# A two-layer convolution kernel: last 3x3 images brought to the points one by one, another order at the start of the 7x7 convolution, sums of two strips

## The chip, the cores and the metric

The kernel runs on one core of one Trainium2 chip. The core has five engines with an instruction queue each: TensorE (PE in the profile; its weight loads are PEld), VectorE (DVE), ScalarE (ACT), GpSimd (POOL) and SyncE (SP), which here only issues DMAs. Each engine works through its queue in order; semaphores make one wait for another. On-chip data lies in SBUF (128 partitions), TensorE writes to PSUM, which has eight banks of 512 float32 values per partition.

The metric is the device time of one execution, in microseconds (us). Times of one kernel agree within about 1%.

## The reference

Everything is float32. The input x is 4 images of 256 channels of 64x64.

```python
# layer 0: attention over 49 shifts
k = conv7x7(x, w1, dilation=2, pad=6) + b1        # 256 -> 128 channels
k = conv1x1(k, w2) + b2                           # 128 -> 49
attn = softmax(k, axis=1)                         # over the 49 shifts
x = sum over u, v in 7x7 of shifted(x, 2u, 2v) * attn[u, v]   # 256 channels
# layer 1: bottleneck with batch statistics
h = relu(bn(conv1x1(x, w1)))                      # 256 -> 64
h = relu(bn(conv3x3(h, w2, pad=1)))               # 64 -> 64
h = bn(conv1x1(h, w3))                            # 64 -> 256
out = relu(h + x)
```

`bn` takes mean and variance over all images and pixels, so every normalisation needs the whole layer before it.

## The kernel before

**7x7 convolution.** The two convolutions of layer 0 are one: the 7x7 weights are multiplied with the 1x1 weights (`product`, L320), so that the output has 49 channels. The seven rows of taps are done by interpolation: the input rows are combined into values at nine points (0, infinity, and plus and minus the four of `PAIRS`, L63), multiplied there, and combined back. The channels are two halves of 128 (`half` 0 and 1), the columns four strips of eight (`NS`, L68). There are five passes over the points (`passes`, L183), each with two values per pixel column (`xi`, i = 0 and 1). A pass visits each strip on VectorE (`visit`, L233, made of `even`, `odd` and `mix`, all through `stt`, L152), and then TensorE runs `column_convs` (L252, matmuls at L263), which adds into the PSUM banks `acc[i][s]` of the strip and its two neighbours. All five passes run for half 0; their sums go to DRAM (`put_aside`, L282). Then they run for half 1: `put_back` (L592) copies the sums into the banks, `column_convs` adds, and `outputs` (L569) combines the two banks of a strip into `logit`, once both neighbours are through.

**The beginning.** `piece(n, b)` (L345) loads some rows of image b and sorts them into `slots`: four copies per piece (`sort_x`, L161, two for each row parity k), all on ScalarE for even b and all on GpSimd for odd b. A ring of four `raw` tiles holds the pieces. `early(n)` (L351) is the visit of the first pass for the output rows that the pieces so far allow; `early(0)` and `early(1)` do all four strips at once, `early(2)` goes by strip. In between, seven products of half 0 fill seven PSUM banks, `bank[0]` to `bank[6]`, and ScalarE and VectorE empty them (L337 to L343). After that come the first `column_convs`, with the products of half 1 between strips 0, 1 and 2, and `apply_factor` (L227), which prepares `slots` for the second pass.

**Softmax and gather.** `exponents` and `shares` make the softmax; `turn` (L549) transposes the shares on TensorE and copies them to `amat` on ScalarE (L567), in the last turns also on VectorE. `load_xt` loads the input in another layout, `shift_xt` (L122) makes a copy shifted by half the partitions, and `gather` (L714) multiplies the two for 16 units of image and quarter. `conv1` (L758) is the first 1x1 convolution.

**3x3 convolution.** `relu1(slot)` (L887) normalises two images. One image of slot 0 is convolved directly (`direct`, L923); the other three are brought to six points along the row (`inputs`, L899, 12 sums on VectorE into the tiles `vs`), multiplied (`products`, L936, twelve matmuls each) and combined back. Each `vs` tile has room for two images. Then come the second normalisation, the moments for the third (L1002 to L1006), and the outputs (L1047 and L1051).

**Order.** In a `manual_schedule` block the engines named keep the order of the program. The first half of the 7x7 convolution is in such a block for VectorE and TensorE, its beginning also for ScalarE and SP, and the turns for VectorE, TensorE, ScalarE and SP. Elsewhere a scheduler sets the order on each engine.

Of the kernel before, what the change touches and what calls it, by code (L numbers as in the profile page):

```python
# [48 lines left out]
P = 128  # L49
# [44 lines left out]
def conv_seq_kernel(ctx: ExitStack, tc: tile.TileContext, xp, xt, w1, b1, w2t, b2, m1t, g1, be1,  # L94
# [63 lines left out]

    zero_rows(slots)

    def sort_x(copy, raw, b, r0, n, dst, w0):  # L161

        d = dst.rearrange("p k (w b e) i -> p k w b e i", b=B, e=Q)
        nw = d.shape[2]
        for k in range(2):
            m = r0 // 2 + (r0 // 2 + 3 + k) % 2
            count = ((r0 + n) // 2 - m + 1) // 2
            i = (m + 3) // 2
            for a in range(2):
                lo = 2 * m + a - r0  # L170
                copy(  # L171
                    d[:, k, :, PLACE[b], 2 * a : 2 * a + 2, i : i + count],
                    raw[:, lo : lo + 4 * count - 3 : 4, PAD + 2 * w0 : PAD + 2 * w0 + 2 * nw].rearrange(
                        "p r (w c) -> p w c r", c=2
                    ),
                )
# [47 lines left out]

        return row

    def apply_factor(t, factor, n, cols=slice(None)):  # L227

        for k in range(2):
            v = t[:, k, cols, :n]  # L230
            stt(v, v, -factor, t[:, k, cols, 1 : n + 1])

# [4 lines left out]
    def strip(s, n=1):  # L237
        return slice(SW * s, SW * (s + n))
# [37 lines left out]
    with ExitStack() as s1:  # L276
# [13 lines left out]
        with ExitStack() as s2:  # L290
# [54 lines left out]
            def piece(n, b):  # L345
                r0, k = PIECES[n]
                raw = rawp.tile([P, 24, WP], F32, tag="raw", name="raw")
                nc.sync.dma_start(out=raw[:, :k], in_=xp[b, :P, r0 : r0 + k, :])
                sort_x(nc.gpsimd.tensor_copy if b % 2 else nc.scalar.copy, raw, b, r0, k, slots, 0)

            def early(n, cols=slice(None), parts=(even, odd, mix)):  # L351

# [8 lines left out]
                if mix in parts:  # L361
                    mix(p, x0, x1)

            bank = [acc[i][s] for s in (2, 3, 0, 1) for i in range(2)]
            with tc.manual_schedule(engines={mybir.EngineType.Activation, mybir.EngineType.SP}):
                for b in range(B):
                    piece(0, b)
                w1a = load_w1(0)
                early(0)
                nc.scalar.copy(b1row, b1sb.to_broadcast([P, P]))  # L370
                nc.tensor.matmul(bank[7][:, :K], b1row, w2sb, start=True, stop=False)
                nc.tensor.matmul(bank[7][:, :K], ones, b2sb, start=False, stop=True)
                nc.scalar.copy(bias, bank[7][:, :K])
                for b in range(2):
                    piece(1, b)
                    product(w1a, 0, b, bank[b])
                for b in range(2, B):
                    piece(1, b)
                early(1, parts=(even,))
                for v in range(2, 5):  # L380
                    if v > 2:
                        piece(2, v - 3)
                    product(w1a, 0, v, bank[v])
                early(1, parts=(odd, mix))
                for v in range(5, K7):
                    piece(2, v - 3)
                    product(w1a, 0, v, bank[v])
                w1b = load_w1(1)
            for s in range(NS):
                early(2, strip(s))  # L390
            u = weights(0, 0)
            column_convs(0, u, True)
            for v in range(4):
                product(w1b, 1, v, bank[v])
                if v == 1:
                    apply_factor(slots, squares[0], NR - 1, strip(0, 2))
            column_convs(1, u, True)
            put_aside(0, 1)
            apply_factor(slots, squares[0], NR - 1, strip(2, 2))
            for v in range(4, K7):  # L400
                product(w1b, 1, v, bank[v - 2])
        for s in range(2, NS):
            column_convs(s, u, True)
            put_aside(0, s)
# [23 lines left out]
        def fill_stage(h):  # L428
            zero_rows(stage)
            for r0 in range(0, H, ROWS2):  # L430
                for b in range(B):
                    raw = rawp.tile([P, ROWS2, WP], F32, tag="raw", name="raw")
                    nc.sync.dma_start(out=raw, in_=xp[b, P:, r0 : r0 + ROWS2, :])
                    sort_x(nc.scalar.copy, raw, b, r0, ROWS2, stage, R // 2 * h)

        def stage_parts(h, strips=range(2)):
            for s in strips:
# [61 lines left out]
    smp = pool(ctx, "smp", 2)  # L499
    outer = pool(ctx, "outerp", 1).tile([P, OUTER], F32, name="outer")  # L500

    logit = outer[:, :LG].rearrange("p (s j v) -> p s j v", s=NS, j=4)
    combs = outer[:, LG : LG + 4 * WS * K].rearrange("p (n v) -> p n v", v=WS * K)
    n_combs = [0]

    pads = [outer[:, LG + PADS * i : LG + PADS * (i + 1)] for i in range(2)] + [arena[:, 11264 : 11264 + PADS]]
    pads = [t.rearrange("p (j w e) -> p j w e", j=4, w=4) for t in pads]
    bias_s = bias.unsqueeze(1).to_broadcast([P, WS, K])

    def columns(s, h):  # L510

        return logit[:, s].rearrange("p j (w k) -> p j w k", k=K)[:, :, 4 * h : 4 * h + 4, :]

    def exponents(s):

# [50 lines left out]
                else:  # L566
                    nc.scalar.copy(dst, src)  # L567

    def outputs(n, p, s):  # L569

        if p is None:
            for i, j, f in ((0, 0, 1.0 / d_zero), (1, 3, 1.0)):
                stt(logit[:, s, j, :], acc[i][s][:, : WS * K], f, logit[:, s, j, :])
            return
        d = 2.0 * p * p
        for q in PAIRS:
            if q != p:
                d *= p * p - q * q
        m, t = (combs[:, 2 * i + n_combs[0] % 2] for i in range(2))
        n_combs[0] += 1  # L580
        nc.scalar.copy(m, acc[0][s][:, : WS * K])  # L581
        nc.vector.tensor_tensor(t, acc[1][s][:, : WS * K], m, ALU.add)
        nc.vector.tensor_tensor(m, m, acc[1][s][:, : WS * K], ALU.subtract)  # L583
        for j in range(4):
            src, dst = (m if j % 2 else t), logit[:, s, j, :]
            if n == 0:
                dst, src = (v.rearrange("p (w k) -> p w k", k=K) for v in (dst, src))
                stt(dst, src, p**j / d, bias_s)
            else:
                stt(dst, src, p**j / d, dst)  # L590
# [10 lines left out]
    with tc.manual_schedule(engines={mybir.EngineType.SP}):  # L601
        for s in range(2):
            put_back(0, s)
        for s in range(NS):
            if s in (1, 2):
                load_ready(s + 1)
                put_back(0, s + 1)
                load_rows(s + 1)
            if s > 1:
                finish_parts(s)  # L610
            column_convs(s, weights(0, 1), False)
            for d in range(s - 1 if s else 0, s + 1 if s == NS - 1 else s):
                outputs(0, PAIRS[0], d)
    for n, (p, factor, left) in enumerate(passes):
        if n == 0:
            continue
# [6 lines left out]
        for s in range(NS):  # L623
            if n == 2:
                apply_factor(slots, factor, NR - 2, strip(s))
            if p is not None:
                visit(slots, strip(s), p, left)
            for d in ([s] if s == 0 else []) + ([s + 1] if s + 1 < NS else []):
                put_back(n, d)
            column_convs(s, u, False)  # L630
            for d in range(s - 1 if s else 0, s + 1 if s == NS - 1 else s):
                outputs(n, p, d)
            if p is None and 0 < s < NS - 1:
                if s == 2:
                    turn(0, 0)
                exponents(s - 1)
                shares(s - 1)
# [18 lines left out]
    with tc.manual_schedule(  # L656
# [5 lines left out]
        turn(1, 0)  # L662
        exponents(3)
        shares(2)
        load_xt(xtiles[1], *units[0], 1)
        turn(1, 1)
        turn(2, 0)
        shares(3)
        turn(2, 1, True)
        turn(3, 0, True)  # L670
        turn(3, 1, True)
    xts[(*units[0], 0)], xts[(*units[0], 1)] = xtiles[:2]
    more_xt(1)

    o = NH1
    w2blk = arena[:, o : o + 6 * P].rearrange("p (n m) -> p n m", m=P)
# [123 lines left out]
        if n + 2 < len(units):  # L800
            more_xt(n + 2)
    conv1(*units[-2], True)
    s_acc.close()


    pb_ = pool(ctx, "pb", 7, PSUM)
    pst = pool(ctx, "pst", 1, PSUM)
    yins = [arena[:, yin_at + C * 4 * i : yin_at + C * 4 * (i + 1)] for i in range(18)]
    yins += [bks.rearrange("p n v -> p (n v)")[:, : C * 4]]
    n_small = [yin_at + C * 4 * 18]  # L810
# [22 lines left out]
        nc.vector.tensor_tensor(sh, beta, sh, ALU.subtract)  # L833
        return sc, sh

    def from_stats(st, gamma, beta):

        mv, m = small(2), small(3)
        nc.vector.bn_aggr(mv, st.rearrange("p n s -> p (n s)"))
        pm = pst.tile([P, 3], F32, tag="pst", name="pm")  # L840
        nc.tensor.matmul(pm[:, :2], pavg_sb, mv, start=True, stop=True)
        nc.tensor.matmul(pm[:, 2:], pdiff_sb, mv[:, :1], start=False, stop=True, skip_group_check=True)
        nc.vector.tensor_copy(m, pm)
# [3 lines left out]
    def from_sums(sums, gamma, beta):  # L847

        t, m = small(2), small(2)
        nc.vector.tensor_reduce(t, sums, AX.X, ALU.add)  # L850
        pm = pst.tile([P, 3], F32, tag="pst", name="pm")
        nc.tensor.matmul(pm[:, :2], pavg_sb, t, start=True, stop=True)
        nc.vector.tensor_scalar(m, pm[:, :2], 1.0 / (B // 2 * H * W), None, ALU.mult)
        nc.vector.scalar_tensor_tensor(m[:, 1:2], m[:, 0:1], m[:, 0:1], m[:, 1:2], ALU.mult, ALU.subtract)
# [15 lines left out]
    for n in range(len(yins)):  # L870
        load_y(n)

    sc1, sh1 = from_stats(st1, bn12[:, 0:1], bn12[:, 1:2])

# [10 lines left out]
    def relu1(slot):  # L887
# [3 lines left out]
        h = h1[slot][:, :, :, :, 1 : T + 1]  # L891
        for a, r in ((0, 0), (1, R)):
            half = slice(a * MID, (a + 1) * MID)
            do(h[half, :, :, r], half)
        for g in range(2):
            for e in (1, 0):
                do(h[:, e::2, g, 1:R])
# [66 lines left out]
    direct(0, 0)  # L964
    inputs(0, slice(1, 2))
    relu1(1)
    products(0, 1)
    inputs(1, slice(0, 2))
    for g in range(2):
        products(1, g)  # L970

# [141 lines left out]
```

## Time and profile before

| | |
|---|---|
| median of 3 runs | 827.38 us (821.28 to 827.96) |
| the profiled execution | 826.64 us |
| its span, first to last instruction | 824.9 us |
| mean granted clock of TensorE | 0.96 |
| TensorE busy | 744.7 us, 90% |
| VectorE busy | 576.7 us, 70% |
| ScalarE busy | 294.9 us, 36% |
| GpSimd busy | 96.0 us, 12% |
| DMA | 150.27 MB, mean 182 GB/s |

The span in stages, as the timeline shows them: loading and the first products to 62.3 us; the first half of the 7x7 convolution to about 274; its second half to 463.9; softmax and turns to 506.5; gather and first 1x1 convolution to 667.8; first normalisation and 3x3 convolution to 740; moments and third normalisation to 774; outputs to the end.

The span in 40 equal slices of 20.6 us, each digit a busy share in tenths (9 is 90% or more):

```profile
PE   0919999999999999979999998999999969879994
DVE  5689979999577999999999764222323232964695
ACT  2430155112641012101111284343433364235497
PEclk9978999999999999989999999999999979898997
DMA  8930188924897893101200112566757587250298
```

And the chain of work that ended last, in shares of the span by engine:

```profile
PE 75%; DVE 10%; ACT 7%; DMA 4%; issue 3%; ACTq 1%; POOL 0%; SPq 0%; DVEq 0%
```

A busy share is a mean over stages with different limits. What an edit is worth is read from the stage in which it lies: which engine works there without a pause, and what ends the others' waits. In the lines of the timeline and the chain, the first number is the start in us from the span's beginning, the second the length, and then come engine, line of the code, operation and tiles.

### The profile page before, as it was taken

The numbers are of one execution on the slowest core, as the hardware profiler recorded it, in microseconds if no ns is written. First come the engines' busy times: TensorE is split into PE (matmuls) and PEld (weight loads), VectorE is DVE, ScalarE is ACT, GpSimd is POOL, SyncE is SP. The second block draws the span as 40 slices with busy tenths as digits, with TensorE's granted clock in tenths as the row PEclk, the third lists the DMA queues.
The fourth block names the chain that finished last, engine by engine and source line by source line (L and its number), as shares of the span: only waits on it lengthen the run. The fifth ranks groups of instructions, "written<-read, shape, count | busy, mean of one in ns | idle before, by whom it ended". The sixth has DMA issues, their size and how long they took to land.

```text
span 824.9 us, 10896 instructions
## 1 busy us (share of the span) xinstructions
PE 744.7 (90%) x4192; PEld 604.9 (73%) x4192; DVE 576.7 (70%) x697; ACT 294.9 (36%) x585; POOL 96.0 (12%) x149
## 2 busy tenths in 40 slices
PE   0919999999999999979999998999999969879994
PEld 0918988888888888768888888888888844338641
DVE  5689979999577999999999764222323232964695
ACT  2430155112641012101111284343433364235497
POOL 5630010001000010000004001222322200000000
PEclk9978999999999999989999999999999979898997
DMA  8930188924897893101200112566757587250298
GB/s 292 349 157 0 40 277 289 387 99 155 291 379 267 340 336 114 49 20 32 58 20 1 57 49 75 192 233 217 246 186 245 182 294 257 90 165 35 96 371 348
DMA packets 58950, 150.27 MB, mean 182 GB/s; under 512 B 7314, under 2 KB 35602, under 8 KB 54546
## 3 DMA queue, kind: packets, MB, share of 16 engines
q1 hardware_dynamic: 48624, 124.34, 42.9%
q10 hardware_dynamic: 10274, 25.23, 7.9%
q8 instruction: 33, 0.54, 0.3%
q14 instruction: 19, 0.16, 0.1%
HBM read 93.81 MB, written 55.74 MB: 181 GB/s over the span
## 4 chain that ended last, share of the span: by engine, by line
PE 75%; DVE 10%; ACT 7%; DMA 4%; issue 3%; ACTq 1%; POOL 0%; SPq 0%; DVEq 0%
PE acc L263 43%; PE acc L732 16%; DVE arena L152 5%; ACT outer L1051 4%; PE acc L766 4%; PE pdirect L930 3%; PE acc L326 3%; PE pconv L942 2%; PE moments L1006 2%; DVE outer L152 2%; DMA raw<-in_xp_dram 1%; PE acc L560 1%; ACT arena L567 1%; DMA bn<-in_g_dram 1%; PE pturn L1002 1%
## 5 line engine op out<-in xcount | busy, mean ns | idle before, releaser
L263 PE MATMUL acc<-arena 128*128 128x343 f32 (+4 forms) x2000 | 381.5, 353 | 25.9 <-DVE arena L152 25.9
L263 PEld LDWEIGHTS acc<-arena 128*128 128x128 f32 x2000 | 322.5, 192 | 83.8 <-issue 21.8
L152 DVE SCALAR_TENSOR_TENSOR arena<-arena 128x1024 f32<-128x1024 f32 (+6 forms) x184 | 292.3, 1626 | 23.6 <-PE acc L263 15.3
L732 PEld LDWEIGHTS acc<-arena,outer 128*128 128x128 f32 x1152 | 130.9, 194 | 9.1 <-issue 6.5
L732 PE MATMUL acc<-arena,outer 128*128 128x128 f32 (+1 forms) x1152 | 132.2, 278 | 2.3 <-ACT arena L567 2.3
L774 DVE BATCH_NORM_STATS2 st<-acc 128x6 f32<-128x512 f32 x16 | 11.1, 694 | 71.6 <-PE acc L766 71.6
L171 ACT COPY stage<-raw 128x128 f32<-128x128 f32 x128 | 43.7, 414 | 22.1 <-DMA raw<-in_xp_dram 20.7
L326 PE MATMUL acc<-powers,w1raw 128*128 128x196 f32 (+1 forms) x196 | 45.6, 396 | 6.0 <-DMA w1raw<-in_w_dram 6.0
L287 ACT COPY sv<-acc 128x392 f32<-128x392 f32 x40 | 19.2, 484 | 85.0 <-PE acc L263 68.9
L326 PEld LDWEIGHTS acc<-powers,w1raw 128*128 128x128 f32 x196 | 44.8, 315 | 6.3 <-DVE arena L152 6.1
L124 ACT COPY outer<-outer 64x2304 f32<-64x2304 f32 x15 | 31.7, 2111 | 31.2 <-DMA outer<-in_xt_dram 26.4
L152 DVE SCALAR_TENSOR_TENSOR outer<-outer 128x392 f32<-128x392 f32 (+3 forms) x67 | 38.4, 631 | 5.0 <-DMA arena<-y_dram 5.0
L989 PE MATMUL pconv<-arena,w3m 64*128 64x512 f32 x128 | 41.8, 638 | 0.0
L581 ACT COPY outer<-acc 128x392 f32<-128x392 f32 x16 | 7.7, 486 | 92.6 <-PE acc L263 73.8
L942 PE MATMUL pconv<-outer,arena 128*128 128x512 f32 x72 | 33.9, 633 | 4.1 <-DVE outer L152 4.1
L754 DVE COPY bks<-acc 128x256 f32<-128x256 f32 x32 | 12.1, 419 | 36.1 <-PE acc L732 36.1
L598 ACT COPY acc<-bks 128x392 f32<-128x392 f32 x40 | 19.3, 491 | 48.5 <-DVE outer L583 29.2
L989 PEld LDWEIGHTS pconv<-arena,w3m 64*128 64x128 f32 x128 | 19.1, 185 | 21.1 <-DVE arena L1047 15.8
L1051 ACT ACTIVATE outer<-arena 128x512 f32<-128x512 f32 x50 | 33.0, 750 | 3.7 <-DVE arena L833 1.4
L1047 DVE SCALAR_TENSOR_TENSOR arena<-pconv,arena 128x512 f32<-128x512 f32 x50 | 33.3, 740 | 0.0
L125 POOL COPY outer<-outer 64x2048 f32<-64x2048 f32 x15 | 28.3, 1885 | 41.3 <-DMA outer<-in_xt_dram 40.3
L567 ACT COPY arena<-acc 128x512 f32<-128x512 f32 x52 | 26.9, 718 | 13.9 <-PE acc L560 13.9
(142 smaller groups left out, 638.9 us busy)
## 6 DMA issues: line engine op xcount, KB each, us to landing
raw<-in_xp_dram SPq DMA_DIRECT2D x36, 608.0 KB, 5.6
out_dram<-outer ACTq DMA_DIRECT2D x16, 1024.0 KB, 4.1
outer<-in_xt_dram SPq DMA_DIRECT2D x17, 896.0 KB, 5.8
arena<-y_dram SPq DMA_DIRECT2D x25, 512.0 KB, 7.8
fsort_dram<-stage SPq DMA_DIRECT2D x2, 4864.0 KB, 15.1
arena<-fsort_dram SPq DMA_DIRECT2D x8, 1216.0 KB, 9.6
y_dram<-outer SPq DMA_DIRECT2D x16, 512.0 KB, 5.1
aside_dram<-sv ACTq DMA_DIRECT2D x40, 196.0 KB, 4.6
```

Source lines behind the costliest of these rows:

```text
L124: nc.scalar.copy(t[:MID], x[MID:])
L152: nc.vector.scalar_tensor_tensor(out, in0, scalar, in1, ALU.mult, ALU.add)
L171: copy(d[:, k, :, PLACE[b], 2 * a : 2 * a + 2, i : i + count], raw[:, lo : lo + 4 * count - 3 : 4, PAD + 2 * w0 : PAD + 2 * w0 + 2 * nw].r ...
L263: nc.tensor.matmul(acc[i][d][:, o : o + (hi - lo) * K], xi[:, i, CW * w : CW * w + CW, :].rearrange("p x t -> p (x t)"), u[i][:, lo * K : ...
L326: nc.tensor.matmul(pw[:, o : o + n], w1raw[:, :, u * K7 + v], powers[:, u, :n], start=(u == 0), stop=(u == K7 - 1), skip_group_check=True,)
L567: nc.scalar.copy(dst, src)
L732: nc.tensor.matmul(pt[:, o : o + hi - lo], x[:, i, half * P : (half + 1) * P], a[:, :, blocks, :].rearrange("p x m e -> p m x e"), start=( ...
L766: nc.tensor.matmul(pt[a * MID : (a + 1) * MID, :], w1m[:, n, :], ys[a, n][:, 512 * i : 512 * i + 512], start=(n == 0), stop=(n == NH - 1), ...
L942: nc.tensor.matmul(m[k], wu[:, k, j, :], vs[k][:, g, j : j + R, :], start=(j == 0), stop=(j == 1))
L989: nc.tensor.matmul(pt, w3m[part, half * P : (half + 1) * P], h2[part, slot, q, 512 * i : 512 * (i + 1)], start=True, stop=True)
L1047: nc.vector.scalar_tensor_tensor(v, conv3(b, q, i, half), sc3[:, half : half + 1], v, ALU.mult, ALU.add)
L1051: nc.scalar.activation(dst, v.rearrange("p (r w) -> p r w", w=R), AF.Relu, bias=sh3[:, half : half + 1])
```

## The change

- **Pieces.** `sort_x` does three of a piece's four copies on ScalarE and the fourth, that of k = 1, a = 1, on GpSimd, for every image. (The later `fill_stage` keeps all four on ScalarE.)
- **Order of the beginning.** `early(1)` does strips 0 and 1 where it did all four; strips 2 and 3 follow after `early(2)` of strip 1. `early(2)` of strip 0 moves up between the last pieces and products. The products of half 0 use the banks in the order of the strips. The products of half 1 stand together after `column_convs` of strip 1, in four banks (strips 3 and 0); `apply_factor` is done for strips 0-1 after the first of them, and for strips 2-3 by parity after the fifth and the seventh.
- **Sums of two strips.** `outputs` works on two strips (g) at once, after the third and the fourth strip of each pass. `logit` is laid out by pairs of strips, `combs` is twice as large, and each instruction has 784 elements instead of 392, with the banks of two strips as its PSUM operand. The last pass stays by strip (`last_outputs`).
- **End of the turns.** The load of the second x tile moves behind `shares(3)`, the next unit's load and shift move into the block with the written order, behind the last turn, and the table of Sqrt is loaded on ScalarE there.
- **First normalisation.** Its two small matmuls write to a bank of `acc`, so the pool `acc` is closed after them; the pool for the 3x3 part has eight banks instead of seven and one.
- **`relu1(0)`.** Its two edge rows are done on VectorE, in two instructions each.
- **3x3.** `inputs(1)` is done image by image: the first ahead of `products(0, 1)`, the second behind it.

```diff
-    def sort_x(copy, raw, b, r0, n, dst, w0):
+    def sort_x(raw, b, r0, n, dst, w0, last=None):
...
-                copy(
+                (last if last and k + a == 2 else nc.scalar.copy)(
...
-            bank = [acc[i][s] for s in (2, 3, 0, 1) for i in range(2)]
+            bank = [acc[i][s] for s in range(NS) for i in range(2)]
+            spare = [acc[i][s] for s in (NS - 1, 0) for i in range(2)]
...
-                early(1, parts=(even,))
+                early(1, strip(0, 2), (even,))
                 for v in range(2, 5):
                     if v > 2:
                         piece(2, v - 3)
                     product(w1a, 0, v, bank[v])
-                early(1, parts=(odd, mix))
-                for v in range(5, K7):
-                    piece(2, v - 3)
-                    product(w1a, 0, v, bank[v])
+                early(1, strip(0, 2), (odd, mix))
+                piece(2, 2)
+                product(w1a, 0, 5, bank[5])
+                piece(2, 3)
+                early(2, strip(0), (even, odd))
+                product(w1a, 0, 6, bank[6])
+                early(2, strip(0), (mix,))
                 w1b = load_w1(1)
-            for s in range(NS):
+            early(2, strip(1))
+            early(1, strip(2, 2))
+            for s in range(2, NS):
                 early(2, strip(s))
             u = weights(0, 0)
             column_convs(0, u, True)
-            for v in range(4):
-                product(w1b, 1, v, bank[v])
-                if v == 1:
-                    apply_factor(slots, squares[0], NR - 1, strip(0, 2))
             column_convs(1, u, True)
             put_aside(0, 1)
-            apply_factor(slots, squares[0], NR - 1, strip(2, 2))
-            for v in range(4, K7):
-                product(w1b, 1, v, bank[v - 2])
+            product(w1b, 1, 0, spare[0])
+            apply_factor(slots, squares[0], NR - 1, strip(0, 2))
+            for v in range(1, 5):
+                product(w1b, 1, v, spare[v % 4])
+            apply_factor(slots, squares[0], NR - 1, strip(2, 2), (0,))
+            for v in range(5, K7):
+                product(w1b, 1, v, spare[v % 4])
+            apply_factor(slots, squares[0], NR - 1, strip(2, 2), (1,))
...
-        nc.scalar.copy(m, acc[0][s][:, : WS * K])
-        nc.vector.tensor_tensor(t, acc[1][s][:, : WS * K], m, ALU.add)
-        nc.vector.tensor_tensor(m, m, acc[1][s][:, : WS * K], ALU.subtract)
+        a0, a1 = (accall[:, 4 * g + i : 4 * g + i + 3 : 2, : WS * K] for i in range(2))
+        nc.scalar.copy(m, a0)
+        nc.vector.tensor_tensor(t, a1, m, ALU.add)
+        nc.vector.tensor_tensor(m, m, a1, ALU.subtract)
...
-            for d in range(s - 1 if s else 0, s + 1 if s == NS - 1 else s):
-                outputs(n, p, d)
+            if p is None:
+                for d in range(s - 1 if s else 0, s + 1 if s == NS - 1 else s):
+                    last_outputs(d)
+            elif s > 1:
+                outputs(n, p, s - 2)
...
         shares(2)
-        load_xt(xtiles[1], *units[0], 1)
         turn(1, 1)
         turn(2, 0)
         shares(3)
+        load_xt(xtiles[1], *units[0], 1)
         turn(2, 1, True)
         turn(3, 0, True)
         turn(3, 1, True)
-    xts[(*units[0], 0)], xts[(*units[0], 1)] = xtiles[:2]
-    more_xt(1)
+        xts[(*units[0], 0)], xts[(*units[0], 1)] = xtiles[:2]
+        nc.scalar.preload_act_table(AF.Sqrt)
+        more_xt(1)
...
-    pb_ = pool(ctx, "pb", 7, PSUM)
-    pst = pool(ctx, "pst", 1, PSUM)
...
-        pm = pst.tile([P, 3], F32, tag="pst", name="pm")
...
-    sc1, sh1 = from_stats(st1, bn12[:, 0:1], bn12[:, 1:2])
+    sc1, sh1 = from_stats(st1, bn12[:, 0:1], bn12[:, 1:2], bank(0)[:, :3])
+    s_acc.close()
+    pb_ = pool(ctx, "pb", 8, PSUM)
...
-            do(h[half, :, :, r], half)
+            if slot:
+                do(h[half, :, :, r], half)
+            else:
+                v = h[half, :, :, r]
+                nc.vector.tensor_scalar(v, v, sc1[half], sh1[half], ALU.mult, ALU.add)
+                nc.vector.tensor_scalar(v, v, 0.0, None, ALU.max)
...
     inputs(0, slice(1, 2))
     relu1(1)
+    inputs(1, slice(0, 1))
     products(0, 1)
-    inputs(1, slice(0, 2))
+    inputs(1, slice(1, 2))
```

## The prediction

> **What bounds the kernel now.** I read the page first (TensorE is busy 90% of the span and carries 75% of the chain), then TensorE's waits, then the chain and the stretches around the longest of them. An edit off TensorE is worth only what it takes out of TensorE's waits or out of the short serial parts between stages. TensorE's waits, all engines' lines by what ended them:
>
> ```profile
> engine line waited for: us in total, times, longest us
> PE acc L263 <- DVE arena L152: 25.9, 4, 17.9
> ...
> PE pdirect L930 <- ACT outer L889: 4.5, 1, 4.5
> PE pconv L942 <- DVE outer L152: 4.1, 1, 4.1
> ...
> PE acc L732 <- ACT arena L567: 2.3, 1, 2.3
> PE pm L841 <- ACT arena L782: 2.1, 1, 2.1
> ```
>
> Five places, and the change touches each. The 25.9 are one wait of 17.9 at 44.4 us (first 7x7 matmul, 62.33) and three of 8.0 together at 348 to 389 us. Between 105.14 and 348.62 TensorE has 1300 matmuls and no wait. The chain across the first wait (start, length, what; merged neighbours, the short links left out):
>
> ```profile
> 30.32 1.67 POOL arena L171 x2
> 32.02 2.69 DVE arena L152
> 34.73 2.53 DVE arena L152
> ...
> 40.62 2.39 ACT arena L171 x3
> ...
> 47.32 1.95 DVE arena L152
> ...
> 57.13 0.65 DVE arena L152
> ...
> 62.33 0.99 PE acc L263 x2
> ```
>
> VectorE (DVE) carries it: three, then five sums over 512x3 elements, then eight over 128x4 for strip 0. The first two take 2.6 us instead of 1.95 because GpSimd copies beside them; GpSimd's copies take 2.6 instead of 0.84. ScalarE (ACT) waits inside it too: `piece(2, 0)` is held until the `even` sums end. The stretches of the 3x3 part, with columns busy time by engine, then TensorE's granted clock, DMA share and GB/s:
>
> ```profile
> core 0: us, PE busy (x) PEld busy (x) DVE busy (x) ACT busy (x) POOL busy (x), PEclk, DMA share, GB/s
> ...
> 674.90:681.00 6.10, 6.06 (x7) 2.47 (x8) 3.80 (x7) 6.01 (x6) 0.00 (x0) 0.50 1.05 387
> 681.00:698.60 17.60, 17.60 (x42) 7.73 (x41) 3.71 (x6) 7.14 (x15) 0.00 (x0) 1.00 0.68 246
> ...
> 712.50:716.60 4.10, 0.04 (x1) 0.00 (x0) 4.10 (x6) 2.03 (x5) 0.00 (x0) 0.82 0.00 0
> 716.60:722.70 6.10, 6.06 (x8) 2.58 (x9) 5.86 (x6) 0.00 (x0) 0.00 (x0) 0.56 0.49 145
> ```
>
> After a pause of 4.1 us the clock is half for 6.1 us: a wait costs its length and 3 us more.
>
> **The change, part by part.**
>
> *Start, 0 to 125 us.* ScalarE now copies three of each piece's four parts and GpSimd one; `early(1)` is cut into strips 0-1 (ahead of the first matmul) and 2-3 (behind strip 1); `early(2)` of strip 0 moves between the last pieces. The pieces arrive when they did (last of the second four at 30.32: the DMA share is 9 tenths or more from 8 us till then). ScalarE, 0.79 us a copy (four in 3.12 to 3.20) and 0.57 per pair of evacuation copies, has 23.56 + 2.4 = 26.0; product 0 to 27.2; then 29.5; product 1 to 30.1; two pieces in, 34.1 for what `even` reads. So `even` starts 2.1 us later than at 32.02. From there, each step from its row: `even` 3 x 1.0 (half the 1.95), plus 0.6 for one GpSimd copy beside it, 37.7; ScalarE's `piece(2, 0)` 2.4, evacuation 0.6, `piece(2, 1)` 2.4, evacuation 0.6, VectorE's pair 0.8, 44.5; `odd` and `mix` 5 x 1.0 + 0.6, 50.1; pair 0.8; six strip-0 sums at 0.72 + 0.4, 55.6; pair 0.8, last two sums 1.4, 57.8. First matmul at 58.0 against 62.33: 4.3 us.
>
> Does it last? VectorE's whole work up to the first visit of the second pass is the same, only reordered: from 57.8, 5.4 + 8 + 10.9 of early sums, seven pairs 5.6, four factor sums of 4.91 us and a wait of 1, 108.9 (now 110.89). TensorE: 58.0 + 11.0 + 10.1 (two strips) + 21.8 (seven products now in a row) + 18.7 (100 of the 1300) = 119.6. The visit's first output is its fifth sum of 2.28: 120.3. TensorE waits 0.7 there, and some 3.6 to 4.0 remain; I take 4.0, as its rates are rounded. The second products have four banks; the sixth needs the second's sums, behind two factor sums: ready 94.0, wanted 94.6, no wait. The second weights load still starts when TensorE ends the first products, 44.5, and has 30 us of cover. Nearest bound for what no row shows (the 256x3 shape): 0.86, as 1024 in a row take 1.16, to 1.3, as beside GpSimd; eight of them, 2.5 to 5.5 us gained.
>
> *Sums of two strips.* Six VectorE instructions of 392 become six of 784 for two strips: 0.48 from start to start (four in 1.99) against 0.89 (two of 784 in 1.85), 0.42 us saved per pair, 1.7 by the largest of the three late waits. Against it: strips 0 and 1 are now summed together, and in the changed order the first pair of a pass stands ahead of visits that the next strips need. In the second pass I count VectorE standing some 3 us before that pair, its banks not yet complete, and strip 3's visit 2 us late. I take +0.3, between -2 and +2. Elsewhere TensorE covers it.
>
> *End of the softmax.* ScalarE's shift copy (2.11 us, behind 1.20 of DMA) stands ahead of the last three turning copies; the gather begins at 506.50 though its transposes end at 504.17. The change puts it behind them: the gather at 504.4, 2.1 us (1.2 to 2.4). The load of the second x tile moves behind the last shares: issued at about 491.6 instead of 486.6, landing 5.8 later at 497.4, 7 us before use; SP's next loads need transposes that end at 498 anyway. The Sqrt table and the shift end ScalarE at 508.2; the second unit is wanted 72 matmuls of 0.113 later, 512.5.
>
> *First normalisation and ReLU.* Now: 669.83 table load 1.28, Sqrt 671.13, ReLU 672.23. The row ends where Sqrt begins. [...] by the row 1.3, and I take the row. Not all is gained: the mean's matmuls move from 669.86 to 669.2 (they no longer wait for ScalarE's last copies to free the banks), so Sqrt can start at 670.45: 0.7 us. Slot 0's two edge ReLUs go to VectorE, four instructions of 64x128, each under the 0.36 of a 128x196, up to 1.4 us beside ScalarE; but in the changed order slot 1's two edges (0.50 each) stand first on ScalarE, so only one of three leaves. Together 1.0 us (0.5 to 1.5); `direct` starts at 673.9. [...] The pause shrinks from 4.47 to some 4.0; the trace kept its clock over 2.33 us (at 504) and lost it over 4.1. [...] I take 0.
>
> *3x3 on points.* `inputs(1)` is cut; its first half goes into the half that slot 0 leaves empty, ahead of `products(0, 1)`. VectorE idles 15.9 us before 700.63, and 12 sums at 0.63 (12 of 528 in 7.52) fit. The second half follows the reads of `products(0, 1)`: 7.6, and 6.8 for that product's sums, done by about 713; wanted at 718. TensorE's 72 matmuls now run 698.64 to 736.68, 38.0; at the full clock's 0.43 they take 31.0. Gain 7.0. With eight banks the first reuse, at 711, needs sums of about 705. If the cover failed, the second half's 7.6 us would come back.
>
> Sum: 4.0 + 0.3 + 2.1 + 1.0 + 7.0 = 14.4, from the profiled run's 826.64 (span 824.9 and 1.7 around it): 812.2. That run is 0.7 under the median of three, 827.38.
>
> **The rivals.** (A) VectorE's unchanged total takes the start back: visits begin nearer 110, the second pass waits, 1.5 remains and the pairs lose 1: 826.64 - 10.6 = 816. For it: only 0.7 us separates the two engines at 120. Against: ScalarE's waits inside VectorE's chain shrink. (B) The 3x3 wait is replaced: [...] gain 2 instead of 7: 817.2. Against: every bank I checked is free 5 us early. (C) Slower: banks held for a pair. A pair's sums free two strips at once, 0.9 on ScalarE, 0.89 + 1.16 + 0.89 on VectorE, 1.0 putting back; the next pass wants the third strip 8.2 us after the pass's end. So it decides once VectorE comes to a pair over 3.4 us late. I count 3.5 at the first, but that strip is used some 4 us into its turn. If every pair's sums were exposed by a strip's 2.9 us, 8 x 2.9 = 23 would outweigh 14.4: 835. (D) Better: the clock survives before `direct` and the pairs give their full 2: 807.5.
>
> **How the numbers follow.** Forecast 0.52, A 0.19, B 0.15, C 0.06, D 0.08. A measurement of this kernel tells about 1% from no change: faster means under 819.1. Forecast, A, D and most of B lie below: 0.85 faster, 0.09 within, 0.06 slower. The range 807 to 818 leaves out C, the worst of B and the edge of D. The time is the forecast's, 812.
>
> **What would show it.** First 7x7 matmul at 58; visits of the second pass from 109, with a TensorE wait under 1 us near 120; waits at 345 to 385 still about 8; gather 2 us nearer the last transpose; no table load at the normalisation; `direct` cold for 6 us; 72 products in 31 us at clock 1.00. A wait of TensorE before `products(1, 0)`, or waits at each pass's second strip, would make it wrong.

## The result, and the profile after

The changed kernel takes 813.62 us (median of 4 runs, 808.99 to 815.58), the kernel before 827.05 (821.28 to 827.96): a ratio of 0.985, with a 95% interval of 0.9825 to 0.988. The forecast was 812. The profiled execution took 815.58 us (span 813.4), so the two profiled spans differ by 11.5 us.

TensorE's waits after, from all engines' lines by what ended them (engine, line, waited for: us in total, times, longest):

```profile
PE acc L263 <- DVE arena L152: 20.6, 3, 11.5
...
PE pdirect L947 <- ACT outer L901: 4.2, 1, 4.2
...
PE acc L746 <- POOL outer L126: 1.8, 1, 1.8
...
PE acc L851 <- DVE arena L850: 1.4, 1, 1.4
PE acc L326 <- DVE arena L343: 1.4, 1, 1.4
```

The wait of the second products (4.1) and the one at the gather (2.3) are gone. The first wait of the 7x7 conv is 11.5 instead of 17.9. But the other two of its three are 5.99 at 365 and a new one: 3.11 us at 119 to 122.

The next table gives the length of each stage, in us of the profiled executions. Its marks are the first 7x7 matmul, the evacuation near 255 us (ScalarE, L287, which waits for the 7x7 matmuls of the first half), the first turning transpose, the averaging matmul of the first normalisation, the first matmul of the direct part and of the products, the averaging matmul of the second normalisation, and the first `pprod`. "Again" is the changed kernel in another execution; "visit first" is an experiment told below.

| to | before | after | again | visit first |
|---|---|---|---|---|
| first 7x7 matmul | 62.33 | 56.08 | 55.66 | 56.39 |
| evacuation near 255 | 193.26 | 200.98 | 198.00 | 195.64 |
| first transpose | 208.15 | 205.97 | 204.96 | 204.85 |
| first averaging matmul | 206.13 | 203.47 | 201.32 | 201.96 |
| direct | 5.07 | 4.81 | 4.81 | 4.81 |
| products | 23.70 | 22.19 | 22.98 | 22.61 |
| second averaging matmul | 41.71 | 34.64 | 34.64 | 34.64 |
| third normalisation | 29.31 | 30.25 | 28.99 | 28.86 |
| end | 55.19 | 55.05 | 55.05 | 55.29 |

The reader is to see two things. The beginning gains 6.25 us and gives back 7.7 before the next mark. And two executions of one kernel differ by 7.0 us in span: by 2.98 between the first matmul and 255, by 2.15 up to the first averaging matmul, by 1.3 ahead of the third normalisation.

VectorE's timeline after shows why it gives back (start, length, engine, line, tiles, count, and in brackets the idle time before, with what ended it):

```profile
33.66 3.89 DVE L152 SCALAR_TENSOR_TENSOR arena<-arena 128x768 f32<-128x768 f32 x3 [3.04 <-ACT arena L171]
...
43.92 5.74 DVE L152 SCALAR_TENSOR_TENSOR arena<-arena 128x768 f32<-128x768 f32 x5
...
50.24 4.43 DVE L152 SCALAR_TENSOR_TENSOR arena<-arena 128x512 f32<-128x512 f32 x6
...
83.17 9.82 DVE L152 SCALAR_TENSOR_TENSOR arena<-arena 128x4608 f32<-128x4608 f32 x2
...
96.92 4.95 DVE L152 SCALAR_TENSOR_TENSOR arena<-arena 128x4608 f32<-128x4608 f32 x1
...
104.89 0.36 DVE L342 TENSOR_TENSOR arena<-arena,acc 128x196 f32<-128x196 f32 x1 [2.36 <-ACT arena L338]
...
105.56 18.78 DVE L152 SCALAR_TENSOR_TENSOR arena<-arena 128x4608 f32<-128x4608 f32 x7
```

The first three lines are the faster beginning (the first sums at 33.66, forecast 34.1). The fourth, fifth and the first instruction of the last line are the four factor sums of 4.9 us; the visits of the second pass follow at about 110.5, where they were before (110.89). A wait of 2.36 stands ahead of the last factor sum. The pair of the seventh product waits for ScalarE's L338, and ScalarE's timeline has that copy behind one that waits for a DMA:

```profile
100.97 0.48 ACT L287 COPY sv<-acc 128x392 f32<-128x392 f32 x1 [0.25 <-PE acc L263]
...
104.31 0.41 ACT L171 COPY stage<-raw 128x128 f32<-128x128 f32 x1 [1.92 <-DMA raw<-in_xp_dram]
104.62 0.24 ACT L338 COPY arena<-acc 128x98 f32<-128x98 f32 x1
```

TensorE comes to the second pass at 119.04 and waits until 122.15. Behind the wait stands the clock. Stretches of the changed kernel, cut where the clock changes (busy time by engine, then TensorE's granted clock, DMA share and GB/s):

```profile
117.89:121.30 3.41, 1.15 (x6) 0.75 (x4) 3.38 (x2) 2.06 (x7) 0.00 (x0) 1.00 0.97 303
121.30:124.72 3.42, 2.57 (x6) 2.16 (x7) 3.39 (x3) 2.61 (x9) 0.00 (x0) 0.50 0.86 245
124.72:128.13 3.41, 3.41 (x8) 2.14 (x7) 3.38 (x2) 1.34 (x5) 0.00 (x0) 0.50 1.00 346
128.13:131.54 3.41, 3.41 (x17) 2.76 (x16) 3.38 (x3) 2.96 (x10) 0.00 (x0) 1.00 0.82 277
671.31:674.30 2.99, 2.99 (x4) 1.39 (x5) 0.73 (x2) 2.99 (x3) 0.00 (x0) 0.50 1.05 387
674.30:693.50 19.20, 19.20 (x46) 8.34 (x46) 14.31 (x23) 9.56 (x17) 0.00 (x0) 1.00 0.85 310
693.50:724.30 30.80, 30.80 (x73) 13.49 (x71) 23.88 (x47) 11.46 (x27) 0.00 (x0) 1.00 0.45 153
```

In this execution the clock is half for 6.8 us, from 121.30 to 128.13 (the last section has such stretches of other profiles). After the wait TensorE works 6.0 us of these and so loses 3.0. With the wait of 1.36 ahead of the sixth product (the L326 line above), that is 1.4 + 3.1 + 3.0 = 7.5 of the 7.7 given back. Further on, the direct part is cold (at half clock) for 3.0 us instead of 6.1, and the products run 72 records without a wait at clock 1.00. The same place in "again", cut in the same lengths:

```profile
117.06:120.47 3.41, 1.53 (x7) 0.97 (x6) 3.38 (x2) 1.35 (x4) 0.00 (x0) 1.00 0.99 364
120.47:123.88 3.41, 2.16 (x9) 1.76 (x10) 3.38 (x3) 2.87 (x9) 0.00 (x0) 1.00 0.96 301
123.88:127.30 3.42, 3.42 (x17) 2.79 (x16) 3.38 (x3) 1.63 (x5) 0.00 (x0) 1.00 0.92 309
```

The pause is the same (3.13 us), but the clock is not lost.

### The profile page after: what moved, and what is told of

It is laid out like the page before. It is cut to its first block, busy times and chain, and to the rows that moved or that the text cites. A ratio compares the mean times of both kernels' runs of the same rounds, so it can differ in the third digit from the quotient of the medians.

```text
span 813.4 us, 10844 instructions
## 1 busy us (share of the span) xinstructions
PE 741.9 (91%) x4192; PEld 604.4 (74%) x4192; DVE 573.7 (71%) x673; ACT 300.4 (37%) x587; POOL 79.3 (10%) x137
## 5 line engine op out<-in xcount | busy, mean ns | idle before, releaser
L263 PE MATMUL acc<-arena 128*128 128x343 f32 (+3 forms) x2000 | 383.9, 355 | 20.8 <-DVE arena L152 20.6
L152 DVE SCALAR_TENSOR_TENSOR arena<-arena 128x1024 f32<-128x1024 f32 (+7 forms) x192 | 290.6, 1560 | 28.0 <-PE acc L263 17.3
L287 ACT COPY sv<-acc 128x392 f32<-128x392 f32 x40 | 19.0, 484 | 103.9 <-PE acc L263 101.7
L326 PE MATMUL acc<-powers,w1raw 128*128 128x196 f32 (+1 forms) x196 | 45.7, 397 | 6.3 <-DMA w1raw<-in_w_dram 4.9
L326 PEld LDWEIGHTS acc<-powers,w1raw 128*128 128x128 f32 x196 | 44.8, 315 | 6.9 <-issue 6.7
L591 ACT COPY outer<-acc 128x784 f32<-128x784 f32 x8 | 6.5, 812 | 101.1 <-PE acc L263 81.2
L152 DVE SCALAR_TENSOR_TENSOR outer<-outer 128x784 f32<-128x784 f32 (+2 forms) x47 | 36.9, 839 | 3.6 <-DMA arena<-y_dram 3.6
L1007 PEld LDWEIGHTS pconv<-arena,w3m 64*128 64x128 f32 x128 | 19.1, 185 | 20.5 <-DVE arena L1065 15.4
L959 PE MATMUL pconv<-outer,arena 128*128 128x512 f32 x72 | 31.1, 592 | 0.0
```

The costliest lines, as they stand in the source:

```text
L152: nc.vector.scalar_tensor_tensor(out, in0, scalar, in1, ALU.mult, ALU.add)
L263: nc.tensor.matmul(acc[i][d][:, o : o + (hi - lo) * K], xi[:, i, CW * w : CW * w + CW, :].rearrange("p x t -> p (x t)"), u[i][:, lo * K : ...
L326: nc.tensor.matmul(pw[:, o : o + n], w1raw[:, :, u * K7 + v], powers[:, u, :n], start=(u == 0), stop=(u == K7 - 1), skip_group_check=True,)
L959: nc.tensor.matmul(m[k], wu[:, k, j, :], vs[k][:, g, j : j + R, :], start=(j == 0), stop=(j == 1))
L1007: nc.tensor.matmul(pt, w3m[part, half * P : (half + 1) * P], h2[part, slot, q, 512 * i : 512 * (i + 1)], start=True, stop=True)
```

## The experiments

Each was timed beside the kernel before, whose median was 826.52 beside `old_start`, `visit_first`, `single_sums` and `inputs_whole`, 825.53 beside `again`, `start_only`, `warm_direct` and `visit_warm`, and 826.02 beside the four whose names begin with `vf`. Ratios are to it, with their 95% intervals. These three groups ran on three chips; as the medians of the kernel before lie up to 1.0 us apart in them, a difference of about 1 us between kernels of two groups says nothing.

**The beginning undone, and alone.** `old_start` is the changed kernel without the first seven hunks (separate pieces) of the diff; `start_only` is the kernel before with them alone. The core of the first as an edit of the changed kernel:

```diff
-                sort_x(raw, b, r0, k, slots, 0, nc.gpsimd.tensor_copy)
+                sort_x(nc.gpsimd.tensor_copy if b % 2 else nc.scalar.copy, raw, b, r0, k, slots, 0)
...
-                early(1, strip(0, 2), (even,))
+                early(1, parts=(even,))
...
-            column_convs(1, u, True)
-            put_aside(0, 1)
-            product(w1b, 1, 0, spare[0])
+            for v in range(4):
+                product(w1b, 1, v, bank[v])
```

> The changed kernel with the beginning of the 7x7 conv as it was before (ScalarE and GpSimd copy whole pieces, early sums over four strips, product and factor order of before); all else as changed. Theory from the two traces: the changed beginning has its first 7x7 matmul 6.25 us earlier but is 1.5 us later from 180 to 272 us, because TensorE then waits 1.36 and 3.11 us and runs about 8 us at half clock. Undone, the first matmul is at 62.3 again, the evacuation that the trace of before has at 255.59 is there again (257.06 in the changed kernel), and the kernel takes 1.5 us less than the changed one: about 812. Rival (the prediction on record): the beginning gives 4.0 us, so undone it costs 4.0: about 817.5. Second rival: the second input half is bound by VectorE and swallows either, 0.

> The kernel before with the changed beginning of the 7x7 conv alone (the first seven hunks of the diff). Prediction on record: 4.0 us less than before, 822.5. Theory: first matmul 6 us earlier, wait of 3.1 us near 119, so from 1.5 us later (clock lost: about 828) to 1.6 us earlier (clock kept: about 825) at 255, that is no difference within 1.6 us. Rival: as the changed kernel without it was 3.7 us under the first times of the changed kernel, it costs 3 to 4 us: 830.

`old_start` took 809.89, ratio 0.980 (0.978 to 0.983): no slower than the changed kernel. `start_only` took 825.42 in 22 runs, ratio 1.0005 (0.9988 to 1.0022): between 1.0 us gained and 1.8 lost. The prediction's 4.0 falls, and so does the rival's loss of 3 to 4. In its profile the first matmul is at 56.29, TensorE waits 1.10 and 3.02, the clock is half for 3.4 us, and the evacuation comes at 255.78 (255.59 before).

**The same kernel again.**

> The changed kernel once more. Three kernels with its beginning have the same wait of 3.1 to 3.2 us at 119 to 122 us, and the clock granted from 119 to 130 was 0.69, 0.84 and 1.00 in them; the evacuation at 257.06 came at 255.77 and 253.93. Theory: a pause of this length loses the clock in some executions and not in others, so the times of this kernel spread over 3 us and more (809 to 816), and its evacuation falls anywhere from 253.9 to 257.1. Rival: the three kernels differ for another reason; then the profile is like the first one, 257.1 within 0.3, and the times lie at 813.6 within 1.

811.21 us (808.56 to 811.85), ratio 0.982 (0.980 to 0.984); the evacuation came at 253.66, against 257.06. The rival falls: the beginning gains 1.9 us when its pause leaves the clock, and loses 1.5 when it takes it for 6.8 us. The other profiles with this beginning fit in: the evacuation comes at 253.93 in `inputs_whole`, where the clock stays; at 255.77, 255.78 and 256.66 in `single_sums`, `start_only` and `warm_direct`, with 3.4 us at half. With the old beginning it comes at 255.59 (before) and 256.06 (`old_start`).

**The second pass's visit first.** `visit_first`:

```diff
-            apply_factor(slots, squares[0], NR - 1, strip(2, 2), (0,))
...
-            apply_factor(slots, squares[0], NR - 1, strip(2, 2), (1,))
...
+                if (n, h) == (1, 1):
+                    apply_factor(slots, squares[0], NR - 1, strip(2, 2))
                 visit(slots, strip(2 * h, 2), p, left)
```

> The changed kernel, with the factor sums of strips 2 and 3 (four instructions, 9.8 us of VectorE) moved from ahead of the second pass's visits to behind the visit of its strips 0 and 1. Theory: VectorE's unchanged work ahead of those visits is what took the start back. Moved, the visit starts near 101 instead of 110.5, TensorE's wait of 3.11 us at 119 and the cold clock behind it go, TensorE is 5 to 6 us ahead of the changed kernel at 255 (251 to 252 against 257.06), and the kernel takes 4 to 6 us less: 808 to 810. Rival: the second input half is bound by VectorE; the late waits of TensorE grow by what it gained, and the time is within 1 us of the changed kernel's. Second rival: VectorE is late instead at strip 2 of the second pass (a new wait there near 138) and half of it comes back.

What moves is two instructions of 4.9 us, 9.8 together; the "four" of the expectation counts those of strips 0 and 1 too. 805.52 us (804.89 to 806.85), ratio 0.9755 (0.973 to 0.978): 5.7 under `again`, and the intervals of the two ratios do not meet. The spread, 3 to 7 us, falls to 2. TensorE's timeline:

```profile
100.45 38.26 PE L263 MATMUL acc<-arena 128*128 128x147 f32 x206
139.49 214.25 PE L263 MATMUL acc<-arena 128*128 128x147 f32 x1138 [0.78 <-DVE arena L152]
359.72 97.32 PE L263 MATMUL acc<-arena 128*128 128x147 f32 x512 [5.98 <-DVE arena L152]
```

There is no pause at 119, and 0.78 us at 139 is all that comes of the second rival. The evacuation is at 252.03, 1.6 us ahead of the one in `again` and 5.0 ahead of the first profile. This version beats both kernels. The wait that took the beginning's gain was set by work that strips 0 and 1 did not need yet.

**Single sums.** `single_sums` is the changed kernel without the four hunks on `logit`, `outputs` and its calls; `vf_single` the same on the base `visit_first`:

```diff
-            elif s > 1:
-                outputs(n, p, s - 2)
+            for d in range(s - 1 if s else 0, s + 1 if s == NS - 1 else s):
+                outputs(n, p, d)
```

> The changed kernel with the sums of each pass's outputs taken strip by strip again (six VectorE instructions of 392 elements for each strip instead of six of 784 for two). Theory from the traces: TensorE went from 1.5 us behind at 272 to 0.7 ahead at the end of the 7x7 conv, so the pairs give 2.2 us; undone, the waits at 345 to 390 are about 8 us or more again and the kernel takes 2.2 us more: about 815.8. Rival (the prediction on record): 0.3 us. Second rival: the 2.2 are only the second half's slack over the late start, and undone it costs nothing, because the later start would have been swallowed as well.

> The same base, with the sums of the outputs taken strip by strip again. Prediction on record: 0.3 us more, 805.8. Theory from the traces of six kernels (time from the evacuation near 255 to the first turning transpose: 208.2 to 208.8 with single sums, 204.1 to 206.1 with pairs): 2.7 us more, 808.2, and TensorE busy 43.4 of the 52 us from 340 to 392 instead of 46.0. Rival: the earlier first half has given VectorE slack, so it costs 0.

`single_sums` took 812.57, ratio 0.984 (0.981 to 0.986): 1.4 over `again`, which the intervals do not part. `vf_single` took 811.38, ratio 0.983 (0.981 to 0.984), 5.9 over its base; between the two profiles the difference is 4.8 in span, 4.2 of it from the evacuation to the first transpose (209.0 against 204.85). With the old beginning that stretch shows nearly the same: 208.15 before, 204.06 in `old_start`, 4.1 less with pairs. TensorE in `vf_single`:

```profile
337.72 8.93 PE L263 MATMUL acc<-arena 128*128 128x147 f32 x44 [0.86 <-DVE arena L152]
348.60 8.91 PE L263 MATMUL acc<-arena 128*128 128x196 f32 x44 [1.95 <-DVE arena L152]
362.45 23.45 PE L263 MATMUL acc<-arena 128*128 128x147 f32 x112 [4.94 <-DVE arena L152]
386.63 75.16 PE L263 MATMUL acc<-arena 128*128 128x147 f32 x400 [0.73 <-DVE arena L152]
```

Four waits, 8.5 us, have become one of 5.98; 2.5 of the 4.2 are that, and the other 1.7 are in part a longer stretch of cold work (6.3 us instead of 4.0, which costs 1.2). Why the long wait is 5.98 or 5.99 in every profile with pairs and the changed beginning, and 4.49 in `old_start`, was not tried.

**Points in one piece.** `inputs_whole`, and `vf_inputs_whole` on the base `visit_first`:

```diff
-    inputs(1, slice(0, 1))
     products(0, 1)
-    inputs(1, slice(1, 2))
+    inputs(1, slice(0, 2))
```

> The changed kernel with the points of slot 1 of the 3x3 conv brought in one piece behind the first products again, VectorE's edges of slot 0 left as changed. Prediction on record and theory agree: TensorE waits some 4 us before the second products and runs 6 us at half clock, 7.0 us more: about 820.6. Rival: with eight banks and the earlier start of the direct part VectorE comes sooner, the wait falls under 2.3 us and the clock stays: 2 to 3 us more.

> The changed kernel with the second pass's visit ahead of the factor sums of strips 2 and 3 (no pause at 119, 805.5 us when it ran), and with the points of slot 1 brought in one piece again. Prediction on record: 7.0 us more, 812.5, with a wait of 4.1 to 4.2 ahead of the second products and 40 records in 19 to 20 us instead of 17.2. Rival, from the first such run (4.2 over the changed kernel, which has the pause at 119 in both): VectorE and the eight banks give part of it back, 4 us more, 809.5.

`inputs_whole` took 815.37, ratio 0.988 (0.985 to 0.991), 4.2 over `again`; `vf_inputs_whole` 813.39, ratio 0.985 (0.983 to 0.987), 7.9 over its base. The profiles of both have the same wait, here that of `vf_inputs_whole` (4.20 in the other):

```profile
685.69 13.89 PE L959 MATMUL pconv<-outer,arena 128*128 128x512 f32 x32
703.78 19.10 PE L959 MATMUL pconv<-outer,arena 128*128 128x512 f32 x40 [4.19 <-DVE outer L152]
```

From the first product to the averaging matmul these kernels take 40.78, the changed one 34.64: 6.1, where the kernel before took 41.71. The difference lies in the clock: 3.4 us at half, where the kernel before had 6.8. So the prediction's cause holds, and the rival of a smaller wait falls (4.2 again). The medians stand 4.2 and 7.9 apart where the profiles of this stage say 6.1. The pause at 119, which kept its clock in the profile of `inputs_whole`, may account for the first; nothing here explains the second.

**The end of the softmax, and the normalisation.** On the base `visit_first`, `vf_old_turn` has the order of the shift and the table load of before, `vf_old_norm` (second part of the diff) the banks and ReLUs of before:

```diff
-        xts[(*units[0], 0)], xts[(*units[0], 1)] = xtiles[:2]
-        nc.scalar.preload_act_table(AF.Sqrt)
-        more_xt(1)
+    xts[(*units[0], 0)], xts[(*units[0], 1)] = xtiles[:2]
+    more_xt(1)
...
-    pb_ = pool(ctx, "pb", 8, PSUM)
+    pb_ = pool(ctx, "pb", 7, PSUM)
+    pst = pool(ctx, "pst", 1, PSUM)
...
-            if slot:
-                do(h[half, :, :, r], half)
-            else:
-                v = h[half, :, :, r]
-                nc.vector.tensor_scalar(v, v, sc1[half], sh1[half], ALU.mult, ALU.add)
-                nc.vector.tensor_scalar(v, v, 0.0, None, ALU.max)
+            do(h[half, :, :, r], half)
```

> The same base, with the shift of the second unit's x tile ahead of the last three turning copies again, and the Sqrt table loaded where it is first used; the second x tile's load stays behind the shares. Prediction on record: the gather comes 2.1 us later, and the table load of 1.28 is back ahead of the first Sqrt (0.7 of it on the path): 2.8 us more, 808.3. Rival: as the load now comes later, the shift waits for it longer (it lands some 5.8 us after its issue at 491), and the copies behind it too: 4 us more and a pause that loses the clock. Second rival: ScalarE's shift is not late any more, 0.

> The same base, with the first normalisation's averaging matmuls in a bank of their own and all ReLUs of slot 0 on ScalarE as before; the Sqrt table stays loaded early. Prediction on record: the whole part gives 1.0 us, of which the table is 0.7 at most; without the rest some 0.5 us more, 806.0, with the pause ahead of the direct part 4.5 to 5 us long. Rival: the seven banks instead of eight hold the products back as well, 2 us more.

`vf_old_turn` took 811.37, ratio 0.982 (0.981 to 0.984): 5.9 over its base, twice the forecast. TensorE stops for 2.40 us and then loses its clock; first the wait, then the stretches around it:

```profile
489.04 7.21 PE L567 MATMUL acc<-ident,outer 128*128 128x128 f32 x64
498.64 21.94 PE L745 MATMUL acc<-arena,outer 128*128 128x64 f32 x180 [2.40 <-ACT arena L574]
```

```profile
495.46:498.87 3.41, 1.01 (x10) 0.77 (x8) 0.73 (x2) 3.35 (x4) 2.66 (x5) 1.00 0.00 0
498.87:502.28 3.41, 3.41 (x18) 3.41 (x18) 1.16 (x2) 0.20 (x1) 0.00 (x0) 0.50 0.00 0
502.28:505.70 3.42, 3.42 (x32) 3.42 (x32) 1.51 (x4) 0.00 (x0) 0.31 (x1) 1.00 0.02 5
```

So in these two profiles the part is worth some 2.4 of wait, 1.7 of cold work, 0.75 of table (from the averaging matmul to direct 5.56 instead of 4.81), and 1.1 in a direct part that is cold for longer. `vf_old_norm` took 805.96, ratio 0.976 (0.974 to 0.978): 0.4 more where 0.5 was forecast, but less than the runs can tell from nothing. In its profile the averaging matmul waits 2.08 instead of 1.42, and the pause is 4.37 instead of 4.21.

**Matmuls in the pause.** `warm_direct` adds four matmuls to the changed kernel, `visit_warm` to `visit_first`:

```diff
+    warm = pb_.tile([P, 512], F32, tag="pb", name="warm")
+    for _ in range(4):
+        nc.tensor.matmul(warm, w2blk[:, 0, :], arena[:, NH1 : NH1 + 512], start=True, stop=True)
```

> The changed kernel with four more matmuls of 512 columns (eight records, some 3.4 us; their result is read by nothing) between the two averaging matmuls of the first normalisation and the direct part of the 3x3 conv. Theory: the pause of 4.2 us ahead of the direct part loses the clock in every run, and its 48 records take 22.4 to 23.9 us instead of the 20.6 of the full clock; with the pause cut under 1 us they take 20.6 to 20.9, and the kernel gains 1.7 to 3.0 us against the changed one. Rival: the clock depends on a longer average than this pause, or the added matmuls run at half clock and end after 671.3, so direct starts later: 0, or 1 us slower.

> Both additions together: the second pass's visit ahead of the factor sums of strips 2 and 3, and the four matmuls ahead of the direct part. Theory: they add, 8 and 2 us under the first times of the changed kernel: about 803.5, with a spread under 2 us as the pause at 119 is gone. Rival: the gain of the second is within the noise, 805.5.

The clock holds, and the direct part's 48 records (a matmul leaves two here: the four added ones are eight records) take 21.1 us, here in `warm_direct`:

```profile
667.43 3.67 PE L888 MATMUL warm<-arena 128*128 128x512 f32 x8 [0.41 <-DVE arena L853]
671.22 21.14 PE L950 MATMUL pdirect<-outer,arena 128*128 128x512 f32 x48
```

From the averaging matmul to the products that is 25.8 us, against 27.8 in `again`. Yet `warm_direct` took 809.93 (0.981, 0.979 to 0.984) and `visit_warm` 806.06 (0.976, 0.974 to 0.978): no gain that can be told. In both profiles the pause ahead of the moments is now followed by 10.2 us of half clock instead of 6.8, and that stage takes 30.0 and 30.2 us instead of 29.0 and 28.9. That explains 1.0 to 1.3 of the 2.0 in these two executions. Whether it would do so in most is open, and so is the rest.

## Why the prediction was right, and where it was not

The total was right, by terms that were wrong in both directions. Only the 3x3 part and the normalisation came as forecast; that the others cancelled is luck.

- *Start, forecast 4.0; `start_only` says 0.* The first half was right: the first matmul came at 56.08, even 1.9 earlier than forecast. The step that failed is "TensorE waits 0.7 there, and some 3.6 to 4.0 remain". The terms written there add up to 108.3 and not to 108.9. VectorE's visits began at 110.5: the "wait of 1" was four waits of 3.4 in all, one of them 2.36, behind a stage copy and its DMA. TensorE came 0.6 us sooner, and 0.7 became 3.1. The pause took the clock as well in four of six profiles, which the sum has nowhere. The "no wait" of the sixth product was 1.36 us. This is rival A's mechanism, with a higher price than rival A gave it.
- *Sums of two strips, forecast +0.3; 2.2 from before to after, 4.2 on the base `visit_first`.* The step that failed is the deduction for VectorE standing ahead of a pair. It stood no longer than before (3.8 us between 303 and 390, by its waits for the sums, against 3.9). The saving of 1.7 by the late waits was about right: they fell from 8.0 to 6.0, and "still about 8" was wrong. This is rival D's full 2. Rival C did not appear.
- *End of the softmax, forecast 2.1; wait 2.4 and clock 1.7.* The prediction said that the trace "kept its clock over 2.33 us (at 504)". It did not. Stretches of the kernel before, cut where the clock changes:

```profile
503.44:506.85 3.41, 1.08 (x10) 0.85 (x9) 0.85 (x2) 3.41 (x4) 2.57 (x5) 1.00 0.00 0
506.85:510.27 3.42, 3.42 (x18) 3.42 (x18) 1.03 (x2) 0.08 (x1) 0.00 (x0) 0.50 0.00 0
510.27:513.68 3.41, 3.41 (x32) 3.41 (x32) 1.51 (x4) 0.00 (x0) 0.31 (x1) 1.00 0.02 5
```

  The gather's first 3.4 us ran at half clock, 1.7 lost, which the prediction left out. A GpSimd shift that TensorE waits for (1.84 us at 563) took the same amount back in the profiled execution after; `again` does not have it.
- *Normalisation and ReLU, forecast 1.0; 0.9 from before to after.* Right: the averaging matmul waits 1.42 instead of 2.08, and from it to direct it is 4.81 instead of 5.07. Undone one at a time, the table and the rest cost 0.75 and 0.8 in the profiles, so they overlap. The clock ahead of direct, taken at 0 as an estimate, gave 1.5 in the profiled execution and 0.3 to 1.1 in others. "Cold for 6 us" was 3.0.
- *3x3 on points, forecast 7.0; 7.1 from before to after in the profiles; undone, 6.1 in two profiles, 4.2 and 7.9 in their medians.* Right, with its cause. Rival B did not appear.
- Between the second averaging matmul and the end 0.8 us were lost, not forecast, with the clock ahead of the moments.

Row by row of the table of stages (the first two rows taken together), what the profiled spans gained is -1.5 + 2.2 + 2.7 + 0.3 + 1.5 + 7.1 - 0.9 + 0.1 = 11.5.

## What to carry to other kernels

When a change brings work forward, add up what the engine that feeds the next stage has still to do, and ask which of it that stage does not need: moving two such sums, 9.8 us of VectorE, was worth more than the whole new beginning. Price a TensorE pause by its length and by the clock behind it, also one of 2.4 us; and as the same pause (of 3.1 us) costs the clock in one execution and not in the next, compare stages over several profiles. A total that fits says nothing of its terms until each is undone alone.

## What the hardware showed

Cut where it changes, the granted clock is 1.00 or 0.50 in all 14 profiles, and the cold stretches that end within the span lasted 3.4, 6.8, 10.2, 13.7, 17.1 or 20.5 us (the last in `old_start`, 46.93 to 67.41). Their lengths in us, by place:

| | 120 | 360 | gather | direct | 2nd products | moments |
|---|---|---|---|---|---|---|
| before | 0 | 6.8 | 3.4 | 10.2 | 6.8 | 10.2 |
| after | 6.8 | 6.8 | 0 | 6.8 | 0 | 10.2 |
| again | 0 | 6.8 | 0 | 6.8 | 0 | 6.8 |
| `start_only` | 3.4 | 6.8 | 3.4 | 10.2 | 6.8 | 10.2 |
| `visit_first` | 0 | 6.8 | 0 | 6.8 | 0 | 6.8 |
| `warm_direct` | 3.4 | 6.8 | 0 | 0 | 0 | 10.2 |

Ahead of each of these stands a pause of TensorE. After pauses of 1.95 us (near 350; before, `start_only`, `single_sums`, `vf_single`) the clock stayed at 1.00; those of 2.24, 2.33 and 2.40 at the gather (`start_only`, before, `vf_old_turn`) lost it, and so did all 30 of 4.1 us or more after the first 7x7 matmul. The pause of 3.0 to 3.2 us at 120 lost it in 4 of 6 profiles. No run shows what tells the four from the other two.
